# Where the window mask is added: two TensorE products a tile, or one VectorE addition in PSUM

## The chip, the cores and the metric

The kernel runs on one core of one Trainium2 chip. The metric is the device time of one execution, in microseconds (us). The time before is the median of three runs. A separate execution, taken with the hardware profiler, gave the profile and the trace. Engines are named as the profile names them: PE is TensorE (PEld its weight loads), DVE is VectorE, ACT is ScalarE, POOL is GpSimd, SP is SyncE, which here only issues DMAs.

## What is computed

The reference first runs a small decoder block over 2 x 512 tokens of width 128 (a Mamba scan, a mixture of experts and a cross-attention), and then six layers of windowed attention with a feed-forward network. The part that this change touches is the mask and the softmax of those six layers:

```python
q, k, v = split(x @ Wqkv)                       # 16 heads of 64
q = l2norm(q) * qs;  k = l2norm(k) * ksc        # then rotary position tables
bk2, bv2 = look(bk), look(bv)                   # windows of 32 tokens, each sees itself and the one before: 64 keys
mask = (it < jb) | (it > jb + w) | (jb == -1)   # later keys, keys over 32 back, keys before the start
sim  = einsum('bhwie,bhwje->bhwij', bq, bk2) * QK_SCALE
sim  = where(mask, -finfo.max, sim)
attn = softmax(sim, -1)
out  = einsum('bhwij,bhwje->bhwie', attn, bv2)  # then @ Wo, the residual and the feed-forward network
```

The mask has the same pattern for every head and every window, but for the first window of a sequence, in which the 32 keys of the window before do not exist.

## The kernel before

The first part (Mamba, experts, cross-attention; to about 376 us of the profile) is not changed, but for two ACT copies in its scan stage, which turn the mask constants into bf16, and one DMA that brings them in.

The six attention layers are cut into 48 tiles: 6 layers x 2 sequences x 4 tiles of 128 tokens (`ti` is the tile's number within its sequence, 0 to 3). Weights and constants lie in SBUF. The order of PE, ACT, DVE and POOL is written out by hand (L1434 to L1527): each engine works strictly in the order in which the steps are issued. Step s of the loop weaves together three tiles and the feed-forward network of a finished sequence:

- tile s, called A: `project` (q, k by PE into PSUM, L965), `rotate` (two DVE products from PSUM, L977 and L981, and a POOL addition, L986), `square` (ACT, L970) and `sums` (DVE, L990), `values` (PE L998, ACT copy to `va` L1000, DMAs to the shifted copy `vb`), `norm` (L1006 to L1015: the inverse square root by ACT's Ln and Exp, L930 and L931, a Newton step on POOL, L932 to L935, and POOL's two products with the rotated q and k, L1012);
- tile s-1, called B_: `flip_q` and `flip_k` (PE transposes L1147, ACT copies L1148), `scores` (L1032 to L1056), `softmax` (L1058 to L1064), `expo` (ACT, L1067);
- tile s-2, called C: `flip_p` (the weights transposed, L1147 and L1148), `attend` (PE L1086), `weigh` (DVE reciprocal L1100 and product L1101), `flip_o` (PE L1116, ACT L1118 and L1120), and, for every second tile, `out` (PE `wo_ps` L1137, DVE addition L1140);
- F1 and F2, the feed-forward network of a sequence whose four tiles are done: mean, variance (L1165), `spread` (L1177), `hidden` (L1216 to L1220), `out` (L1239), and ACT's table loads (L938 and L1204). They fall in three of each four steps.

PE's order within a step is: projection of q, flip_q, projection of k, flip_p, flip_k, attend, (hidden), values, scores, flip_o, (variance), (feed-forward out), attention out. While the first four steps run, pieces of the first part's end (`late(1)`) are woven between.

PSUM comes from two pools: "a", three buffers of two banks each (qk_ps, v_ps, sim, av), and "b", two buffers (transposes and outputs). Scores of a tile are a [128, 2, 4, 2, 64] tile of "a": 128 query rows, 16 heads, 64 keys.

`scores` first writes the mask: for each half of the PSUM tile, a product of `hot` (32 x 128 bf16, which says which of the 32 rows of a window a partition is) with `masks` (32 x 512 bf16) opens the accumulation with start=True (L1039). Then 64 small products of q and k, each 32 queries x 64 keys, are added to it with start=False (L1050). For ti = 0 the first of the two mask products takes the variant that also closes the first window's missing keys. `softmax` takes the maximum over the 64 keys (DVE, L1061) and subtracts it on the way from PSUM to SBUF (DVE, L1063); `expo` is ACT's Exp. The last tiles' work is finished by a written-out tail (L1530 to L1590).

Of the kernel before, what the change touches and what calls it, by code (L numbers as in the profile page):

```python
# [11 lines left out]
F32 = mybir.dt.float32  # L12
U32 = mybir.dt.uint32
I32 = mybir.dt.int32
BF16 = mybir.dt.bfloat16
# [6 lines left out]
B, S, D = 2, 512, 128  # L22
NT = B * S
P = 128
# [6 lines left out]
DEPTH, H, DH, WIN = 6, 16, 64, 32  # L31
# [5 lines left out]
NEG = -1e30  # L37
# [12 lines left out]


K_MASK = 0
K_HOT = K_MASK + 1024
K_HM1 = K_HOT + 128
K_HM2 = K_HM1 + 16
K_LT = K_HM2 + 128
K_TRI = K_LT + 64
# [9 lines left out]
def decoder_kernel(ctx: ExitStack, tc: tile.TileContext, t: dict, out: bass.AP):  # L67
    nc = tc.nc
    mm, tr = nc.tensor.matmul, nc.tensor.transpose

    const = ctx.enter_context(tc.tile_pool(name="const", bufs=1))
# [3 lines left out]
    lwb = ctx.enter_context(tc.tile_pool(name="lwb", bufs=1, side="right"))  # L75
# [11 lines left out]
    mhalf = const.tile([P, 1], F32, name="mhalf")  # L87
    nc.gpsimd.memset(mhalf, -0.5)

    hot = const.tile([WIN, P], BF16, name="hot")  # L90
    masks = const.tile([WIN, 2, S], BF16, name="masks")
    xT = const.tile([P, NT], F32, name="xT")

    tri = const.tile([P, P], BF16, name="tri")
# [13 lines left out]
    ps = front.enter_context(tc.tile_pool(name="fps", bufs=1, space=PSUM))  # L108
# [13 lines left out]
    def load(pool, shape, name, src):  # L122
        w = pool.tile(shape, F32, name=name)
        nc.sync.dma_start(out=w, in_=src)
        return w
# [11 lines left out]
    w_dt = load(sp, [DTR, DI], "w_dt", t["L0_attn_dt_proj_w"])  # L137
    cst = const.tile([P, NCST - K_HM1], F32, name="cst")
    nc.sync.dma_start(out=cst, in_=t["cst"][:, K_HM1:])
    stage = lwb.tile([WIN, K_HM1], F32, tag="wqkv", name="stage")  # L140
    nc.sync.dma_start(out=stage, in_=t["cst"][0:WIN, 0:K_HM1])
    w_o = load(fp, [P, 2, D], "w_o", t["L0_attn_out_proj_w"].rearrange("(c p) f -> p c f", p=P))
    w_r = load(fp, [P, NE], "w_r", t["L0_attn_router_w"])
    ctok = load(fp, [B * XK, D], "ctok", t["ctx_1024"].rearrange("b k d -> (b k) d"))
# [231 lines left out]
    def small(name, shape, dtype=F32, bufs=1):  # L376
        return ep.tile([P, *shape], dtype, tag=name, name=name, bufs=bufs)

    def sort(b):
# [12 lines left out]
        gt, eq = small("gt", [NTB, NE, NE]), small("eq", [NTB, NE, NE])  # L392
        lt = cst[:, K_LT - K_HM1 : K_LT - K_HM1 + 64].unsqueeze(1).to_broadcast([P, NTB, 64])
        eqv = eq.rearrange("p n e f -> p n (e f)")
# [418 lines left out]
    with tc.manual_schedule(engines={ET.PE, ET.Activation, ET.DVE, ET.Pool, ET.SP}):  # L813
        xn = norm_in(0)
        nc.scalar.activation(acol, cols[:, C_ALOG : C_ALOG + 2 * NS], AF.Exp)
        nc.gpsimd.tensor_scalar(acol, acol, -1.0, None, ALU.mult)
        turn_in(0, xn)
        xn = norm_in(1)
        p0, p1 = conv(0, 0), conv(0, 1)
        for hf, pm in enumerate((p0, p1)):  # L820
            nc.scalar.activation(xi[0][:, hf], pm, AF.Silu, bias=col(C_CONVB + hf))
        p0, p1 = gate(0, 0), gate(0, 1)
        for hf, pm in enumerate((p0, p1)):
            nc.scalar.activation(sz[0][:, hf], pm, AF.Silu)
        table("natural_log_exp_and_others")
        dt_b_c(0)
        turn_in(1, xn)
        halves = [delta(0, hf) for hf in range(2)]
        for g in halves:
            step(g)  # L830
        for hf, g in enumerate(halves):
            step(g)
            nc.vector.tensor_mul(dx[0][:, hf], dl[0][:, hf], xi[0][:, hf])

        def other_batch():

            p0, p1 = conv(1, 0), conv(1, 1)
            yield
            yield
            table("silu_and_others")  # L840
            for hf, pm in enumerate((p0, p1)):
                nc.scalar.activation(xi[1][:, hf], pm, AF.Silu, bias=col(C_CONVB + hf))
            p0, p1 = gate(1, 0), gate(1, 1)
            for hf, pm in enumerate((p0, p1)):
                nc.scalar.activation(sz[1][:, hf], pm, AF.Silu)
            table("natural_log_exp_and_others")
            yield
            yield
            dt_b_c(1)
            yield  # L850
            nc.scalar.copy(hot, stage[:, K_HOT : K_HOT + P])
            nc.scalar.copy(masks, stage[:, K_MASK : K_MASK + 2 * S].rearrange("p (a s) -> p a s", a=2))
            nc.scalar.copy(tri, cst[:, K_TRI - K_HM1 : K_TRI - K_HM1 + P])
            yield
            for hf in range(2):
                g = delta(1, hf)
                step(g)
                yield
                yield
                step(g)  # L860
                yield
            nc.gpsimd.tensor_mul(dx[1], dl[1], xi[1])

        third = {n for n in range(NS) if n % 3 == 2}
        weave(scan(0, third), other_batch())
        table("exp_and_others")
        e0, e1 = experts(0), experts(1)
        early = chain(route(0), sort(0), e0, combine(0), cross(0))
        beside = [0, 1, 3, 5, 7, 8, 10, 11, 13, *range(16, 32, 2)]
        tables = cross_tables()  # L870
        for i, _ in enumerate(scan(1, {n for n in range(NS) if n % 2 == 0})):
            if i in beside:
                step(early)
            elif i > 14:
                step(tables)
        for _ in tables:
            pass
        scans.close()
        lwa = ctx.enter_context(tc.tile_pool(name="lwa", bufs=1))
        for i, _ in enumerate(chain(route(1), sort(1), e1)):  # L880
            step(early)
            if i in (12, 14, 16, 18, 20):
                step(early)
        for _ in early:
            pass
# [56 lines left out]
    class Tile:  # L942
# [89 lines left out]
        def scores(self):  # L1032

            qT, kT = self.qT, self.kT
            ps = psa.tile([P, 2, 4, 2, 64], F32, tag="a", name="sim")
            for par in range(2):
                mm(  # L1039
                    ps[:, par].rearrange("p g s k -> p (g s k)"), hot,  # L1040
                    masks[:, 1 if self.ti == par == 0 else 0, :],
                    start=True, stop=False, skip_group_check=True,
                )
            for hg in range(4):
                for slot in range(2):
                    for c in range(2):
                        for par in range(2):
                            for r in range(2):
                                j, w = 2 * c + (r ^ par), 2 * slot + par
                                mm(  # L1050
                                    ps[32 * j : 32 * j + 32, par, hg, slot, :],
                                    qT[64 * r : 64 * r + 64, 2 * hg + c, WIN * w : WIN * (w + 1)],
                                    kT[64 * r : 64 * r + 64, 2 * hg + c, WIN * w : WIN * (w + 2)],
                                    start=False, stop=True, skip_group_check=True,
                                )
            self.ps = ps  # L1056

        def softmax(self):  # L1058
            p3 = self.ps.rearrange("p a g s k -> p (a g s) k")
            m = tmp.tile([P, 16], F32, tag="m", name="m")  # L1060
            nc.vector.tensor_reduce(m, p3, AX.X, ALU.max)  # L1061
            s = tmp.tile([P, 16, 64], F32, tag="s", name="s", bufs=1)
            nc.vector.tensor_sub(s, p3, m.unsqueeze(2).to_broadcast([P, 16, 64]))  # L1063
            self.sf = s.rearrange("p x k -> p (x k)")  # L1064
# [369 lines left out]
    with tc.manual_schedule(engines={ET.PE, ET.Activation, ET.DVE, ET.Pool}):  # L1434
        onto_z(0, xT[:, bs(0)])
        rest = late(1)
        for s in range(len(tiles)):
# [93 lines left out]
        a, b, c = (  # L1531
            Part(DEPTH - 1, 1, layers[DEPTH - 1], t0, w)
            for t0, w in ((0, 2 * P), (2 * P, P), (3 * P, P))
        )
# [78 lines left out]
def _cst():  # L1613
    c = np.zeros((P, NCST), np.float32)
    p = np.arange(P)
    q, key = np.arange(WIN), np.arange(64)

    off = q[:, None] + WIN - key[None, :]
    m = np.where((off < 0) | (off > WIN), NEG, 0.0)

    m = np.broadcast_to(m[:, None, None, None, :], (WIN, 2, 4, 2, 64)).copy()
    m[:, 1, :, 0, :WIN] = NEG
    c[:WIN, K_MASK : K_MASK + 1024] = m.reshape(WIN, 1024)
    c[:WIN, K_HOT : K_HOT + P] = q[:, None] == (p % WIN)[None, :]
    c[p, K_HM1 + p // 8] = 1.0
    c[:, K_HM2 : K_HM2 + P] = (p[:, None] % XH) == (p[None, :] // 8)
    e = np.arange(NE)
    c[:, K_LT : K_LT + 64] = (e[None, :] < e[:, None]).reshape(1, 64)
    c[:, K_TRI : K_TRI + P] = (p[:, None] < p[None, :]) / P
    c[:, K_ROW : K_ROW + P] = p[None, :] / P  # L1630
    c[:, K_NUM : K_NUM + NSL] = np.arange(NSL)[None, :]
    c[:, K_TOK] = p
    c[:, K_TOK + 1 : K_TOK + 5] = P * np.arange(4)[None, :]
    return c
# [83 lines left out]
```

## Time and profile before

| what | value |
|---|---|
| runs | 1294.85, 1301.05, 1294.79 us; median 1294.85 |
| the profiled execution | 1302.94 us; its span 1301.2 us |
| mean granted clock of PE | 0.942 |
| 0 to 376 us, first part | PE busy 277 us, DVE 249, ACT 130, POOL 190; clock 0.85 |
| 376 to 456 us, first tiles with the woven end of the first part | PE 61 of 80 us, DVE 57; clock 0.85 |
| 456 to 1223 us, tiles | PE 728 of 767 us; DVE 538, ACT 439, POOL 442; clock 1.00 |
| 1223 to 1302 us, the end | PE 40 of the first 44 us, 24 of the last 35 |
| mask products (L1039) | 96 of 384 ns, two a tile |
| scores (L1050) | 6144 PE records, 1.42 us a tile on the chain of waits |

A "busy" figure is the time in which an engine ran any instruction. In a group's row come the line, the engine, the operation, the tiles out<-in, the shape and the count; then the busy time, the mean time of one in ns, and the idle time of the engine just before it with what ended it. "issue" is time in which an engine waited for nothing that the profile shows. The chain of waits is the sequence of work that ended last, followed back from the end of the execution.

### The profile page before, as it was taken

Reading aid. Unit: us, or ns where it says so; the run is one execution under the profiler, and the core shown is the slowest. Engines: PE = TensorE matmul, PEld = TensorE weight load, DVE = VectorE, ACT = ScalarE, POOL = GpSimd, SP = SyncE. Lnnn points to the kernel's source line nnn. Section 1 sums busy time; section 2 is a strip of 40 time slices with the busy share of each in tenths; the row PEclk is TensorE's granted clock in tenths of the full one; section 3 lists DMA queues with packets and bytes.
Section 4 is the critical chain, followed back from the end, with each engine's and each line's share of the span. In section 5 each row is a group of like instructions: output and inputs, shape, how many; then the busy total and the mean of one; then the engine's idle time right before and its main releaser. Section 6 shows DMA issues by size and latency. Waiting matters only on the chain.

```text
span 1301.2 us, 37984 instructions
## 1 busy us (share of the span) xinstructions
PE 1130.2 (87%) x16629; PEld 733.6 (56%) x16629; DVE 885.0 (68%) x1198; ACT 639.0 (49%) x1126; POOL 695.0 (53%) x704
## 2 busy tenths in 40 slices
PE   6677678857857899999999999999999999899987
PEld 2223256756734666666656666666656565555666
DVE  2798867535587676777767676777767675766654
ACT  4534132313333456565656555565646555554643
POOL 2577574154352565646646464656646464555641
PEclk9888689869977999999999999999999999999998
DMA  3222364468310212111121112111121111101100
GB/s 114 75 65 81 120 194 149 125 185 275 109 46 18 73 40 80 36 45 41 36 79 51 30 40 79 52 42 34 30 79 52 31 35 31 36 18 31 36 15 18
DMA packets 51889, 88.52 MB, mean 68 GB/s; under 512 B 7086, under 2 KB 23852, under 8 KB 51724
## 3 DMA queue, kind: packets, MB, share of 16 engines
q1 hardware_dynamic: 46796, 76.78, 19.6%
q10 hardware_dynamic: 3456, 6.29, 1.7%
q0 software_dynamic: 1472, 3.02, 1.1%
q8 instruction: 131, 2.15, 0.7%
q14 instruction: 34, 0.28, 0.1%
HBM read 58.92 MB, written 3.19 MB: 48 GB/s over the span
## 4 chain that ended last, share of the span: by engine, by line
PE 60%; ACT 9%; DVE 8%; issue 5%; POOL 5%; DMA 0%; another core or an unknown queue 0%; POOLq 0%; DVEq 0%; ACTq 0%
PE qk_ps L965 11%; PE t_ps L1147 7%; PE wo_ps L1137 7%; PE v_ps L998 6%; PE av L1086 4%; PE sim L1050 4%; ACT pT L1148 2%; PE fo_ps L1239 2%; PE t_ps L1116 2%; PE gu_ps L542 2%; PE fg_ps L1216 2%; PE sim L1039 2%; ACT oT L1118 1%; PE fa_ps L1217 1%; ACT sq L970 1%
## 5 line engine op out<-in xcount | busy, mean ns | idle before, releaser
L986 POOL TENSOR_TENSOR t<-t,t 128x1024 f32<-128x1024 f32 x94 | 222.7, 2371 | 155.3 <-DVE t L981 154.3
L965 PE MATMUL qk_ps<-wqkv,z 128*128 128x512 f32 x384 | 187.4, 612 | 0.8 <-ACT sq L970 0.4
L1012 POOL TENSOR_TENSOR t<-t,rn 128x1024 f32<-128x1024 f32 x94 | 177.2, 1907 | 3.7
L977 DVE TENSOR_TENSOR t<-qk_ps,tab 128x1024 f32<-128x1024 f32 x96 | 117.5, 1224 | 76.0 <-PE qk_ps L965 75.9
L1147 PE MATMUL t_ps<-ident,t 128*128 128x128 f32 x768 | 102.8, 277 | 25.0 <-ACT pT L1148 10.8
L1147 PEld LDWEIGHTS t_ps<-ident,t 128*128 128x128 f32 x768 | 87.1, 143 | 63.4 <-issue 36.5
L990 DVE TENSOR_REDUCE ss<-sq 128x16 f32<-128x1024 f32 x96 | 116.4, 1213 | 4.0 <-ACT sq L970 0.2
L1009 POOL TENSOR_SCALAR ss<-ss 128x32 f32<-128x32 f32 x47 | 13.4, 285 | 196.8 <-ACT sc L1008 196.8
L981 DVE TENSOR_TENSOR t<-qk_ps,tab 128x1024 f32<-128x1024 f32 x96 | 116.6, 1215 | 0.0
L1148 ACT COPY qT<-t_ps 128x512 f32<-128x512 f32 x96 | 51.7, 588 | 126.8 <-PE t_ps L1147 126.7
L1061 DVE TENSOR_REDUCE m<-sim 128x16 f32<-128x1024 f32 x48 | 58.8, 1225 | 69.5 <-PE sim L1050 69.5
L970 ACT ACTIVATE sq<-qk_ps 128x1024 f32<-128x1024 f32 x96 | 97.7, 1036 | 12.8 <-DVE t L981 12.8
L965 PEld LDWEIGHTS qk_ps<-wqkv,z 128*128 128x128 f32 x384 | 69.6, 197 | 52.6 <-issue 49.6
L998 PE MATMUL v_ps<-wqkv,z 128*128 128x512 f32 x192 | 93.8, 611 | 0.0
L1137 PE MATMUL wo_ps<-oT,wo 128*128 128x256 f32 (+1 forms) x400 | 89.5, 378 | 3.3 <-ACT oT L1118 3.3
L1086 PE MATMUL av<-va,pT 64*32 64x65 f32 x3072 | 83.9, 228 | 8.9 <-issue 8.9
L314 PE MATMUL y<-hs,ident 128*128 128x512 f32 x128 | 77.4, 741 | 15.5 <-DVE hs L334 9.4
L293 ACT ACTIVATE da<-dl,acol 128x512 f32<-128x512 f32 x64 | 43.8, 690 | 88.5 <-DVE hs L326 60.0
L1086 PE MATMUL av<-vb,pT 64*32 64x65 f32 x3072 | 83.1, 228 | 2.9 <-DVE ln_xc L1198 2.4
L1137 PEld LDWEIGHTS wo_ps<-oT,wo 128*128 128x128 f32 x400 | 73.7, 194 | 19.5 <-ACT oT L1118 6.3
L542 PE MATMUL gu_ps<-xT,w 128*128 128x128 f32 x480 | 72.1, 303 | 11.6 <-ACT xT L535 4.0
L1148 ACT COPY pT<-t_ps 128x512 f32<-128x512 f32 x96 | 51.6, 589 | 62.0 <-PE t_ps L1147 62.0
(351 smaller groups left out, 2323.5 us busy)
## 6 DMA issues: line engine op xcount, KB each, us to landing
w<-in_experts_dram SPq DMA_DIRECT2D x90, 256.0 KB
vb<-va SPq DMA_DIRECT2D x48, 390.0 KB
wqkv<-in_L_ffn_Wqkv_dram SPq DMA_DIRECT2D x18, 512.0 KB
vb<-va SPq DMA_DIRECT2D x36, 130.0 KB
b_sb<-bcd SPq DMA_DIRECT2D x16, 256.0 KB
b_sb<-bcd ACTq DMA_DIRECT2D x16, 256.0 KB
wo<-in_L_ffn_Wo_dram SPq DMA_DIRECT2D x6, 512.0 KB
c_sb<-bcd ACTq DMA_DIRECT2D x8, 256.0 KB
```

The lines of the kernel that those rows point to most:

```text
L965: mm(pa[:, hf * S : (hf + 1) * S], self.xb, w[:, w0 : w0 + S], start=True, stop=True)
L970: nc.scalar.activation(sq.rearrange("p h d -> p (h d)"), self.raw[qk], AF.Square)
L977: nc.vector.tensor_mul(t1, pa.rearrange("p (h d) -> p h d", d=DH), tab[:, 2 * qk, ti, :].unsqueeze(1).to_broadcast([P, H, DH]),)
L981: nc.vector.tensor_mul(t2.rearrange("p h (x d) -> p h x d", x=2), swap_halves(pa), tab[:, 2 * qk + 1, ti, :].rearrange("p (x d) -> p x d", ...
L986: self.calc.tensor_add(t1, t1, t2)
L990: nc.vector.tensor_reduce(self.ss[:, qk], self.sq[qk], AX.X, ALU.add)
L998: mm(pv[:, hf * S : (hf + 1) * S], self.xb, w[:, w0 : w0 + S], start=True, stop=True)
L1012: self.calc.tensor_mul(self.rot[qk], self.rot[qk], self.rn[:, qk].unsqueeze(2).to_broadcast([P, H, DH]),)
L1086: mm(po[hh][32 * at : 32 * at + 32, g, i * DV : (i + 1) * DV], pT[rows, 4 * par + hg, 32 * j : 32 * j + 32], (self.v if par else self.v2)[ ...
L1137: mm(po, wo_l[:, c, :], self.oT[:, c, at : at + w], start=c == 0, stop=c == INNER // P - 1)
L1147: tr(pt[:, n, :], src[:, (4 * g + n) * P : (4 * g + n + 1) * P], ident)
L1148: nc.scalar.copy(dst[:, 4 * g : 4 * g + 4, :], pt)
```

## The change

The mask is no longer a product. The two mask products a tile are gone from `scores`, and each of the 64 score products now writes PSUM by itself (start=True). `softmax` gains one DVE addition ahead of the maximum, in place in PSUM: the scores plus a mask tile from SBUF, read again for every head by a broadcast. For ti > 0 the same 64 values of a partition serve all 16 groups; for ti = 0 the form with 128 values in each half is used, where the first window's mask has the missing keys closed. The constants change with it: `masks` is now [128, 2, 2, 64] in f32, loaded from HBM by one DMA (128 x 256 values), in the place of the DMA of the bf16 masks' f32 source (32 x 1152 values); the ACT copies that made `hot` and `masks` are gone. In the two kernels as built, the orders of instructions on all engines agree otherwise: PE has 96 products and 96 weight loads fewer, DVE 48 additions more, ACT two copies fewer, POOL the same, SP the one DMA replaced.

The Newton step on POOL, which the change's title names as well (`self.calc`, L932 to L935), is in both kernels.

```diff
-    hot = const.tile([WIN, P], BF16, name="hot")
-    masks = const.tile([WIN, 2, S], BF16, name="masks")
+    masks = const.tile([P, 2, 2, 64], F32, name="masks")
...
-    stage = lwb.tile([WIN, K_HM1], F32, tag="wqkv", name="stage")
-    nc.sync.dma_start(out=stage, in_=t["cst"][0:WIN, 0:K_HM1])
+    nc.sync.dma_start(out=masks, in_=t["cst"][:, 0:K_HM1].rearrange("p (a s k) -> p a s k", a=2, s=2))
...
-            nc.scalar.copy(hot, stage[:, K_HOT : K_HOT + P])
-            nc.scalar.copy(masks, stage[:, K_MASK : K_MASK + 2 * S].rearrange("p (a s) -> p a s", a=2))
...
             ps = psa.tile([P, 2, 4, 2, 64], F32, tag="a", name="sim")
-            for par in range(2):
-                mm(
-                    ps[:, par].rearrange("p g s k -> p (g s k)"), hot,
-                    masks[:, 1 if self.ti == par == 0 else 0, :],
-                    start=True, stop=False, skip_group_check=True,
-                )
...
-                                    start=False, stop=True, skip_group_check=True,
+                                    start=True, stop=True,
...
         def softmax(self):
             p3 = self.ps.rearrange("p a g s k -> p (a g s) k")
+            if self.ti:
+                nc.vector.tensor_add(
+                    p3, p3, masks[:, 1, 0].unsqueeze(1).to_broadcast([P, 16, 64])
+                )
+            else:
+                p4 = self.ps.rearrange("p a g s k -> p a g (s k)")
+                nc.vector.tensor_add(
+                    p4, p4,
+                    masks.rearrange("p a s k -> p a (s k)").unsqueeze(2).to_broadcast([P, 2, 4, 128]),
+                )
             m = tmp.tile([P, 16], F32, tag="m", name="m")
             nc.vector.tensor_reduce(m, p3, AX.X, ALU.max)
```

More of the change, by code (lines that the diff above doesn't have):

```diff
@@ L52 @@
 K_MASK = 0
-K_HOT = K_MASK + 1024
-K_HM1 = K_HOT + 128
+K_HM1 = K_MASK + 256
 K_HM2 = K_HM1 + 16
@@ L1619, in _cst @@
     m = np.where((off < 0) | (off > WIN), NEG, 0.0)
[L1621 to L1624, printed above, removed]
+    m = np.broadcast_to(m[:, None, None, :], (WIN, 2, 2, 64)).copy()
+    m[:, 0, 0, :WIN] = NEG
+    c[:, K_MASK : K_MASK + 256] = np.tile(m.reshape(WIN, 256), (P // WIN, 1))
     c[p, K_HM1 + p // 8] = 1.0
```

## The prediction

> **What bounds the kernel now.** I read the table of engines first, then the windows of the tile stage, the chain of waits, DVE's groups and last PE's idle time.
>
> ```profile
> PE 1130.2 (87%) x16629; PEld 733.6 (56%) x16629; DVE 885.0 (68%) x1198; ACT 639.0 (49%) x1126; POOL 695.0 (53%) x704
> PE 60%; ACT 9%; DVE 8%; issue 5%; POOL 5%; DMA 0%; another core or an unknown queue 0%; POOLq 0%; DVEq 0%; ACTq 0%
> ```
>
> The window of the tile stage (stretch, its length, then busy us and instructions of PE, weight loads, DVE, ACT, POOL, and the clock):
>
> ```profile
> 456.00:1223.00 767.00, 727.87 (x13366) 472.80 (x13349) 537.99 (x617) 438.64 (x732) 441.52 (x465) 1.00 0.15 44
> ```
>
> PE is busy 727.87 of 767 us, 95%, at the full granted clock (1.00); DVE 538, 70%. So PE sets the pace, and PE work that goes is worth time wherever nothing else ends just behind it. What goes (L1039), and the rows nearest to what comes, in the groups by shape (busy us, mean ns | idle before):
>
> ```profile
> L1101 DVE TENSOR_TENSOR o<-av,rd 128x512 f32<-128x512 f32 x96 | 66.4, 692 | 3.3
> ...
> L1061 DVE TENSOR_REDUCE m<-sim 128x16 f32<-128x1024 f32 x48 | 58.8, 1225 | 69.5 <-PE sim L1050 69.5
> L1063 DVE TENSOR_TENSOR s<-sim,m 128x1024 f32<-128x1024 f32 x48 | 58.8, 1224 | 1.7
> ...
> L1039 PE MATMUL sim<-masks,hot 32*128 32x512 bf16 x96 | 29.2, 384 | 0.0
> ```
>
> The chain of waits over one tile (start, us, what):
>
> ```profile
> 606.64 1.91 POOL t L1012
> ...
> 608.60 1.09 PE t_ps L1147 x8
> ...
> 613.94 1.43 PE av L1086 x87
> 615.37 1.91 PE v_ps L998 x4
> 617.28 0.53 PE sim L1039 x2
> 617.81 1.42 PE sim L1050 x91
> ```
>
> The mask pair stands on the chain with 0.53 us. Once in four tiles the chain leaves PE: POOL's L1012 releases the flips (L1147).
>
> **Removed from PE.** 96 mask products. A pair lengthens the chain by 0.53, so at most 48 x 0.53 = 25.4 us. With its two weight loads a pair is four of PE's instructions; one event semaphore a tile comes in: counted in the two built programs, 147 less in all, about 3 a tile. This small count matters below.
>
> **Added on DVE.** 48 adds of 128x1024, PSUM plus an SBUF mask into PSUM. The nearest row reads PSUM and SBUF in one pass: L1063, 1.224 us. No row has DVE writing PSUM. Lower bound: the fixed part hidden. L1101 and L1063 give (1224-692)/512 = 1.04 ns an element and 0.16 us fixed, so 1.06. Upper bound: read and write in turn, 2x1.06+0.16 = 2.29. I take 1.22, as its shape is L1063's, and 1.26 with the gap between two DVE instructions. Scores end 0.53 earlier, so the softmax ends 1.26-0.53 = 0.73 later. The add waits for the last score; the maximum, subtraction, DVE's next rotations (L977, L981) queue behind it, expo (L1067) waits for them, and PE's flip_p for expo. The Trainium skill's page "VectorE: DVE Perf Modes", section "Rules for kernel authors", speaks against this: in a chain of DVE operations count matters, for each drains. By it the add costs DVE its full 1.2 us, never the 1.06; by the rows the cost is only what its followers can't wait for. So, by kind of tile (n mod 4):
>
> - n=1 and n=3: DVE is idle 4.1 and 6.7 us before the next rotation, and L1012 ends 4.1 and 5.8 us before flip_q needs it. All hidden: 0.53 gained each.
> - n=2: the timeline of one such tile, DVE's and ACT's, is tight.
>
> ```profile
> 638.67 1.22 DVE L1063 TENSOR_TENSOR s<-sim,m 128x1024 f32<-128x1024 f32 x1
> 641.45 1.22 DVE L977 TENSOR_TENSOR t<-qk_ps,tab 128x1024 f32<-128x1024 f32 x1 [1.56 <-PE qk_ps L965]
> ```
>
> ```profile
> 640.27 1.04 ACT L1067 ACTIVATE s<-s 128x1024 f32<-128x1024 f32 x1
> 641.32 1.28 ACT L1204 ACT_TABLE_LOAD   x1
> ```
>
> L1063 ends at 639.89, with the add at 640.62, so expo starts 0.35 late (not 640.27); ACT's table load and flip_q's copies queue behind it, so flip_p starts at about 643.7 instead of 643.84. Gained: 0.14. The 1.56 idle before L977 absorbs the rest.
> - n=0: PE waits for va, Newton and L1012 (above), none of which moves against v_ps. Gained: 0. The first rotation comes 0.58 later, inside the 1.09 us that DVE idles before the second. Without that cover it would cost up to 0.58.
>
> One group of four gains 0.53+0.14+0.53 = 1.20. Tiles 5 to 47 are 10.75 groups: 12.9. The first four tiles run with PE waiting on the earlier part: net -0.1. The last tile's tail is bound by DVE: +0.7. Sum: -12.3 us. POOL is no worse beside more DVE work: L1012 takes 1.90 both beside the softmax and beside L977.
>
> **Setup.** Two ACT copies of the scan stage go (0.28 and 1.04 us at 52 us): ACT waits there for DVE afterwards, so 0. The mask DMA takes the place of the staging DMA in SP's queue, 128 KB for 144 KB: 0, since it is needed 300 us later; no other queue is passed.
>
> **What moves: PE's instruction pages.** PE's idle time in the waits view names no engine:
>
> ```profile
> PE av L1086 <- issue: 6.0, 4, 1.5
> PE sim L1050 <- issue: 4.9, 4, 1.6
> PE t_ps L1116 <- issue: 3.6, 4, 1.4
> ```
>
> ```profile
> 1116.05 0.21 PE L1086 MATMUL av<-va,pT 64*32 64x65 f32 x1 [1.48 <-issue]
> ```
>
> Counting PE's instructions in the trace, the stalls of the tile stage fall at numbers 15041, 17601, 20161, 22465, 24001 ... 31425: every one is 193 plus a multiple of 256. The instruction queue (q8) moved 131 packets, 2.15 MB, 16 KB each, one for each 256 of PE's 33,603 instructions. Each packet starts about 0.9 us after PE enters a page, and PE resumes some 2.5 us after that: a page that PE runs through in under 3.4 us stalls. The weighted values (256 instructions in 1.4 to 1.75 us) and the scores (1.42) do; a page of scores, flips and products takes longer. There are 14 such stalls of 0.4 to 1.7 us, 17.4 us. The Trainium skill's "Runtime: NRT & Kernel Launch", section "Instruction fetch mechanics", says that crossing a 16 KiB boundary costs a tail-bump, mostly hidden. By the page this term is 0 before and after, and the sum stays -12.3; by the trace it is 17.4 us of before and can change.
>
> Before, a group of four tiles is 2569 instructions, 10 pages and 9: the boundaries drift, so almost pure pages come up only now and then, from tile 20 on. After, it is 2557, 10 pages less 3: the boundaries nearly stand still, and where they stand decides. In the built program of after they stand badly. In all eleven n=1 tiles a page holds 227 to 256 products of attend (L1086): about 1.5 us each. The page behind it (rest of attend, v_ps, some 240 scores) lost 0.8 to 1.0 before and runs 0.5 shorter now: about 0.4 over the eleven. The n=3 tiles 7 to 31 have such a page too (237 to 255), about 1.1 each, and two later ones 0.5. Pages that split attend and scores in halves take 3.3 us: about 0.1 in 22 tiles. Sum: 16.5+4.4+7.7+1+2.2 = 31.8. What goes: 14 stalls, of which 14.3 lengthened their tiles' periods, and one drop of the clock behind a stall, 1.8: 16.1. Net +15.7.
>
> **Sum.** -12.3+15.7 = +3.4 on the profiled execution: 1302.94 us, its span 1301.2 and 1.7 around it, hence 1306.3. The median of the runs is 1294.85, 8.1 lower, perhaps because fetches are faster unprofiled. Both terms carried over, the stalls a little smaller: 1294.85+3 = 1298. With stalls half as large, +7.9-12.3 = -4: 1290.5.
>
> **Rivals.** First, nothing lasting stalls: page costs hide, as the skill has it, or the stalls belong to profiling. Then 1294.85-12.3 = 1282.5; if DVE's add hides everywhere, down to 1270. For it: PE's 95%. Against: 14 rows at exact multiples of 256.
>
> Second, slower: the standing pages stall in full on every attend in the n=1 and n=3 tiles. Place: the boundary before L1086. Price: 22 x 1.5 and 11 x 1.0 on the page behind = 44, less 16.1 and 12.3: +15.6 at worst, and +7 with the n=3 pages at half size; between them 1306. It decides from about 19 full stalls in all on (12.3+16.1 = 28.4 us at 1.5): fewer, and the change gains. Any clock drop behind a stall adds 1.8.
>
> Third: the add in place runs at 2.29. The extra 1.07 costs 0.93 at n=2 and, past 0.52 of cover, 0.55 at n=0, so a group is slower by 1.48-1.06 = 0.4 and stalls come on top: about 1314. Against: L1063 shows no cost for two operands.
>
> Fourth, it doesn't do what it says: excluded, as the built program has 48 more TensorTensor on DVE and 96 fewer matmuls.
>
> **How the numbers follow.** Likeliest, gain and stalls nearly cancelling (1290 to 1303): 0.50. Stalls hidden (1270 to 1288): 0.24. Full stalls (1302 to 1310): 0.20. Slow add (over 1308): 0.06. The range 1281 to 1307 leaves out half of the last two and the far end of the second. A measurement of this kernel can tell about 0.5% (6.5 us) from no change. Faster by more (under 1288.4): 0.25, the second case; slower (over 1301.3): 0.33, the last two and the upper end of the first; within: 0.42.
>
> **What would show it.** DVE's new row: 48 at about 1.22; over 1.6 speaks for the third. PE's busy time falls by about 25 us. The "issue" rows grow from 17 us to about 32, all at multiples of 256 plus 193, attend's in n=1 tiles first; if they don't, this step is wrong. "L1147 <- POOL L1012" stays at once in four tiles. The forecast fails if unprofiled fetches are much faster, or if DVE's later softmax makes PE wait in n=1 or n=3.

## The result and the profile after

The changed kernel takes 1302.05 us (median of 15 runs), the kernel before 1294.85. The ratio of all runs is 1.0047, with a 95% interval of 1.0025 to 1.007: slower by about 6 us (the two medians lie 7.2 apart). It lies in the forecast range (1281 to 1307 us), at the upper edge of the likeliest case (1290 to 1303).

The page of the changed kernel's profile: the span, then the busy time of each engine.

```profile
span 1296.5 us, 37894 instructions
...
PE 1118.8 (86%) x16533; PEld 732.1 (56%) x16533; DVE 942.8 (73%) x1246; ACT 637.7 (49%) x1124; POOL 694.7 (54%) x704
```

This profiled execution is 4.7 us *shorter* than the one of before, although the runs are longer. The two parts of the trace tell why. Scores of the first tile begin at 378.3 us in the trace of before and at 367.4 in this one; the kernels are alike up to there but for the constants, and over the eleven traces of this study that moment lies anywhere between 364.8 and 381.5 us. That part scatters from execution to execution, and only the stretch from the first score to the end belongs to the change. The windows of that stretch, before and then after (length, then busy us of PE, weight loads, DVE, ACT, POOL, and the clock):

```profile
378.29:1301.17 922.88, 852.97 (x15440) 560.59 (x15440) 634.09 (x796) 507.38 (x856) 503.18 (x544) 0.98 0.15 42
```

```profile
367.36:1296.48 929.12, 839.12 (x15346) 559.58 (x15346) 693.32 (x844) 506.98 (x856) 502.56 (x544) 0.98 0.14 42
```

PE is busy 13.9 us less, and the stretch is 6.2 us longer, which is what the runs say (0.0047 x 1295 = 6.1). So PE stands idle 20 us more. (A fall of about 25 us was forecast; the mask products did go, but scores take 4.9 us more in sum, the v_ps products 3.1 and the transposes 2.5.) The groups by shape show the new DVE operation, and the waits of PE from 366 us on show the idleness:

```profile
L1061 DVE TENSOR_REDUCE m<-sim 128x16 f32<-128x1024 f32 x48 | 58.8, 1224 | 1.7
L1063 DVE TENSOR_TENSOR s<-sim,m 128x1024 f32<-128x1024 f32 x48 | 58.8, 1224 | 1.6
...
L1051 DVE TENSOR_TENSOR sim<-sim,masks 128x1024 f32<-128x1024 f32 x36 | 44.4, 1232 | 31.1 <-PE sim L1040 31.0
...
L1056 DVE TENSOR_TENSOR sim<-sim,masks 128x1024 f32<-128x1024 f32 x12 | 14.8, 1231 | 25.9 <-PE sim L1040 25.9
```

```profile
PE av L1086 <- issue: 17.0, 13, 2.4
PE sim L1040 <- issue: 15.3, 12, 4.1
PE t_ps L1147 <- POOL t L1008: 13.0, 12, 2.4
```

The addition in place costs 1.23 us, like its neighbours. The maximum (L1061) had 69.5 us of idle time before it, waiting for scores; now it follows the addition at once. PE's two largest waits are of the kind "issue"; 4.1 us of the scores' row are the gap ahead of the very first score. Counted at the places where PE's instruction number is 193 plus a multiple of 256, so where one page of 256 instructions ends and the next begins, there are 26 gaps of over 0.2 us, 29.8 us in all, for 14 and 17.4 before. These are called stalls here. One of them on the chain of waits:

```profile
608.38 1.36 PE av L1086 x83
609.74 2.37 issue
612.11 0.32 PE av L1086 x8
612.43 3.15 PE v_ps L994 x4
615.58 1.69 PE sim L1040 x100
```

PE stands still for 2.37 us in the middle of attend, and what follows takes 3.15 us where it took 1.91 in the chain of before: the slower pace behind some stalls that the prediction counted once. It is the clock, as the windows around it show (the number behind POOL's is the granted share):

```profile
608.00:612.00 4.00, 1.72 (x122) 1.35 (x121) 2.36 (x4) 2.27 (x4) 4.00 (x2) 1.00 0.12 37
612.00:616.00 4.00, 3.89 (x47) 1.54 (x49) 2.02 (x3) 0.38 (x1) 0.06 (x1) 0.62 0.01 4
```

In the trace's clock record it stands at half for 3.41 us from 612.96 on. Of after's stalls from the fifth tile on, those of 2.37, 2.13 and 2.09 us have such a drop behind them, and one of 2.31 has none.

Tiles are counted from 1 here, so n=1 is the first tile of a sequence. The period of a tile runs from its first score to that of the next tile; the attend that comes just ahead of a tile's first score thus lies in the period of the tile before. The periods by kind of tile, where no stall falls in them (us):

| tile n mod 4 | before | after, undisturbed | forecast gain | gain |
|---|---|---|---|---|
| 1 | 18.04 | 17.51 | 0.53 | 0.53 |
| 2 | 20.40 | 20.13 | 0.14 | 0.27 |
| 3 | 19.69 | 19.15 | 0.53 | 0.54 |
| 0 | 14.00 | 14.00 | 0 | 0 |

### The profile page after: what moved, and what is told of

It reads as the page before. It is cut to its first block, busy times and chain, and to the rows that moved or that the text cites. A ratio compares the mean times of both kernels' runs of the same rounds, so it can differ in the third digit from the quotient of the medians.

```text
span 1296.5 us, 37894 instructions
## 1 busy us (share of the span) xinstructions
PE 1118.8 (86%) x16533; PEld 732.1 (56%) x16533; DVE 942.8 (73%) x1246; ACT 637.7 (49%) x1124; POOL 694.7 (54%) x704
## 3 DMA queue, kind: packets, MB, share of 16 engines
q8 instruction: 130, 2.13, 0.7%
## 4 chain that ended last, share of the span: by engine, by line
PE 58%; DVE 13%; ACT 11%; issue 5%; POOL 4%; DMA 1%; SPq 0%; POOLq 0%; DVEq 0%; ACTq 0%
PE qk_ps L961 8%; PE t_ps L1147 7%; PE wo_ps L1137 7%; PE v_ps L994 7%; PE av L1086 5%; PE sim L1040 4%; PE gu_ps L540 3%; ACT pT L1148 2%; PE fo_ps L1239 2%; PE y L312 2%; POOL t L1008 2%; PE fg_ps L1216 2%; PE xd L561 2%; PE fa_ps L1217 1%; PE t_ps L1116 1%
## 5 line engine op out<-in xcount | busy, mean ns | idle before, releaser
L1008 POOL TENSOR_TENSOR t<-t,rn 128x1024 f32<-128x1024 f32 x94 | 176.8, 1902 | 3.7
L1147 PE MATMUL t_ps<-ident,t 128*128 128x128 f32 x768 | 103.7, 278 | 32.5 <-POOL t L1008 13.0
L1147 PEld LDWEIGHTS t_ps<-ident,t 128*128 128x128 f32 x768 | 86.4, 143 | 71.8 <-issue 32.6
L994 PE MATMUL v_ps<-wqkv,z 128*128 128x512 f32 x192 | 96.8, 627 | 1.7 <-ACT kT L1148 1.1
L1040 PEld LDWEIGHTS sim<-kT,qT 64*32 64x32 f32 x6144 | 66.9, 107 | 54.1 <-issue 52.1
L1040 PE MATMUL sim<-kT,qT 64*32 64x64 f32 x6144 | 77.9, 230 | 16.1 <-issue 15.3
L1067 ACT ACTIVATE s<-s 128x1024 f32<-128x1024 f32 x48 | 50.8, 1058 | 82.1 <-DVE s L1063 82.1
```

Source lines behind the costliest of these rows:

```text
L994: mm(pv[:, hf * S : (hf + 1) * S], self.xb, w[:, w0 : w0 + S], start=True, stop=True)
L1008: self.calc.tensor_mul(self.rot[qk], self.rot[qk], self.rn[:, qk].unsqueeze(2).to_broadcast([P, H, DH]),)
L1040: mm(ps[32 * j : 32 * j + 32, par, hg, slot, :], qT[64 * r : 64 * r + 64, 2 * hg + c, WIN * w : WIN * (w + 1)], kT[64 * r : 64 * r + 64, 2 ...
L1147: tr(pt[:, n, :], src[:, (4 * g + n) * P : (4 * g + n + 1) * P], ident)
```

## The experiments

The theory to be tested: the change gains about 1.3 us in four tiles, and loses it again because it moves the 256-instruction pages of PE to where they stall. The rivals: the stalls belong to profiling, or DVE's later softmax is what the runs pay for. A third, that any idle product at the start changes the time, wherever the pages stand, is tested by the last two runs. The lever is a number of idle products on PE. They write PSUM that a later product overwrites, and put nothing else in another order; each is four PE instructions.

```diff
+    def pads(pt, n):
+        for k in range(n):
+            j = 32 * (k % 4)
+            mm(pt[j : j + 32, 0:64], ident[0:64, 0:32], ident[0:64, 0:64], start=True, stop=True)
...
         pt = bank(name)
+        if name == "nT_ps0":
+            pads(pt, 42)
```

**168 instructions (a168).** 

> The kernel after, with 42 idle products (168 PE instructions, [64x32] by [64x64] of the identity, into PSUM that the first transposes overwrite) at PE's start, where it waits 8 us for its first data. Nothing else moves, but every boundary of PE's pages of 256 instructions stands 168 instructions earlier in the tiles: between halves of attend and scores, no longer at their ends. Page theory: of some 27 stalls (30 us in the trace of after) all but a few go, stalls left under 5 us, time about 25 to 28 below after: ratio to before about 0.983 (1273 us). Rival, the stalls belong to profiling or the added DVE operation is what costs: ratio as after, 1.0047, within 0.3%.

Measured: 1.0333 (1.0305 to 1.0362), slower by 37 us than after, where I had expected 25 faster. The rival allowed 0.3% around after, so it fell; but so did my rule for where the stalls fall. There were 45.9 us of stalls. (A gap of 3.84 us in the first tile also stands at such a number, but it is the wait for kT that the kernel before has there too.) PE's waits in this kernel (attend is now L1093, scores L1047):

```profile
PE av L1093 <- issue: 29.2, 19, 1.9
PE sim L1047 <- issue: 21.4, 18, 4.0
```

The chain of waits of one n=2 tile shows a page that my rule called safe:

```profile
479.23 0.86 PE ln_mean L1160 x2
480.08 0.88 PE t_ps L1154 x8
480.96 1.72 PE qk_ps L968 x4
482.68 0.45 PE t_ps L1154 x4
...
483.15 0.59 ACT pT L1155
...
483.88 1.06 PE t_ps L1154 x8
484.94 0.25 PE av L1093 x8
...
485.20 1.11 PE av L1093 x68
486.32 1.36 issue
487.67 0.46 PE av L1093 x30
```

PE entered this page at 478.63 and left it at 486.32: 7.7 us, far over my 3.4. Yet its packet on the instruction queue started only at 485.35, 6.7 us after the entry and not 0.9; PE resumed 2.3 us after that. No other instruction packet was moved in the 9 us before it, so the request was late, not the queue busy. Here a page of slow transposes and then attend asked late and ran out early.

The clock adds to it. Over tiles 5 to 46 a168 takes 34.1 us more than after. Its gaps are 20.3 us longer, and its granted clock stands at half for 37.5 us, in nine drops behind gaps of 1.6 to 1.9 us, for 6.8 us in after; at half speed the 30.7 us more are worth about 15 (my estimate).

**96 instructions (a96, the same edit with 24 products).** 

> The same with 24 idle products (96 instructions). By the page theory the boundaries now leave the n=1 and n=3 tiles and stand at the ends of attend in the n=2 and n=0 tiles: about as much stalls as in after (26 us worked out from its trace), in other tiles. n=0 waits for POOL anyway and hides part: ratio to before 0.998 to 1.006. Rival, the idle products themselves help or hurt (a warmer clock, a later start): then it goes the way of the run with 168, at about 96/168 of its size.

Measured: 1.0102 (1.0059 to 1.0145), above the expected 0.998 to 1.006, with 34.0 us of stalls. They moved to the n=2 and n=0 tiles as expected. The rise over after is 0.55%, where the rival, by the number of products, makes it 1.6%.

**The kernel before with 112 + 88 instructions (b112j88; flip takes a count and calls pads on its first PSUM tile).** 

> The kernel before, with 28 idle products at PE's start (112 instructions) and 22 more (88) ahead of flip_q of tile 29, where PE waits for POOL anyway. By the page theory its drifting boundaries then miss the attend and score bursts: 14 stalls become about 3, 17 us about 3, and the clock drop goes: ratio to before 0.988 to 0.990 (about 1280 us). Rival: no change, 1.000. Against the run of after with 168 it gives the worth of the change without stalls: after should be 10 to 13 us below (0.990 to 0.992) if the sum without stalls was right, equal if the DVE addition eats the gain.

Measured: 1.0159 (1.0132 to 1.0186), with 24 stalls of 32.3 us instead of 3. The same wrong rule: its boundaries stood in pages of flips and attend.

**168 instructions without the addition (n168).** 

> The run with 168, with the DVE additions left out: no mask is applied at all. It prices the added operation where it stands. My sum: 0 in n=1 and n=3 tiles, about 0.25 to 0.4 in n=2, 0 in n=0, 0.7 to 1.3 in the tail: 3 to 5 us below the run with 168. Rival, the addition is on the path of every tile: 48 x 1.26 less 48 x 0, up to 60 us below.

Measured: 1.0248 (1.0214 to 1.0282), 0.85% or 11 us below a168, with 50.5 us of stalls: too much stands on the stalls for a price of the addition. Inconclusive, but 60 us are excluded.

From these six traces I read off, for each kind of tile, how far from the first score a boundary stalls: where attend and its weights' flips lie. The next runs used these zones, so they test them on kernels from which they were not read.

**56 instructions (a56, 14 products).** 

> The kernel after with 14 idle products (56 PE instructions) at PE's start. The traces of the six kernels so far show where a page boundary stalls: at distances of -55 to 0 instructions from the first score in n=1 tiles, -81 to 13 in n=2, -99 to 13 in n=0 (the flips ahead of attend delay the fetch as well), some at -55 to -30 in n=3. A shift of 56 keeps all four kinds out of these zones but for the first n=0 tiles. Revised page theory (the place of the boundary decides, the place is to be read from traces): stalls in the tiles 1 to 3 us instead of 27, time 22 to 26 us below after: ratio to before 0.984 to 0.988. Rival (any idle products at the start slow the kernel down, as all four did so far): above 1.0047.

Measured: 0.9803 (0.9778 to 0.9829), 1268.0 us. This is 2.4% below after, a little more than expected, and faster than the kernel before: the version that beats both. (Part of its lead over before are before's own 17.4 us of stalls.) The window from its first score to the end, and PE's "issue" waits:

```profile
372.43:1272.30 899.87, 832.39 (x15346) 557.21 (x15346) 693.05 (x844) 507.83 (x856) 502.63 (x544) 0.98 0.15 43
```

```profile
PE sim L1047 <- issue: 5.1, 4, 4.2
PE t_ps L1123 <- issue: 4.4, 3, 2.0
```

The same 844 DVE and 15,346 PE instructions as in after take 29.3 us less. (4.2 us of the scores' row are again the gap ahead of the first score.) What stalls are left (9.6 us) lie mostly in n=0 tiles, where PE would have waited for POOL: from the eighth tile on their period stays 14.0 but for one of 14.19; only the fourth tile's is longer, 16.41. Of the 29.1 us that tiles 5 to 46 lose, 18.3 are gaps and about 3.4 the two drops of the clock, which are gone; the other 7 I did not trace.

**The kernel before with jumps (bj: no products at the start, 34 ahead of flip_q of tile 17 and 17 ahead of that of tile 33).** 

> The kernel before with no products at the start, but 34 idle products (136 instructions) ahead of flip_q of tile 17 and 17 (68) ahead of that of tile 33, chosen by the same zones so that its drifting boundaries miss them. Revised page theory: of 14 stalls (17 us) one or two are left, ratio to before 0.986 to 0.990. Against the run of after with 56, without stalls in either, after should be lower by the gain of the mask products alone, 12 to 14 us (about 1%). Rival, the change is worth nothing or costs without stalls: both equal.

Measured: 0.9974 (0.9958 to 0.999). Eight stalls of 9.4 us were left, for the one or two expected; four of them, of 1.26 to 1.68 us before the n=2 tiles 18, 22, 26 and 30, stand 87 to 114 instructions ahead of the first score, further out than my zone reached. In tiles without stalls its periods are those of before (18.03, 20.40, 19.68, 14.00); the 17 products ahead of tile 33 cost nothing, and the period with the 34 is 14.99, with a stall of 0.30 in it. The run missed its range, so the table above gives the gain without stalls better than these two times do.

**56 instructions without the addition (n56).** 

> The run with 56 without the DVE additions: no mask is applied. It prices the addition with hardly any stalls around: by the periods of the trace of after, 0.25 a tile in n=2 and 0 in the others, and 0.7 to 1.3 in the tail: 3 to 5 us below the run with 56 (ratio to it 0.996 to 0.998). Rival, DVE's later softmax is on the path in most tiles: 10 us or more below.

Measured: 0.9769 (0.9742 to 0.9797), 0.35% or 4.4 us below a56, by the two medians 5.4; the two intervals overlap, so the size is rough, but 10 us would be too much. Of the undisturbed periods only that of n=2 falls, from 20.13 to 19.88: 2.8 us over its eleven tiles from the sixth on. The rest is not where I had put it. The tail, from the last tile's first score on, does not fall (39.34 and 39.50 us in the two traces). The second tile does, from 26.51 to 24.48 (with 168 instructions from 25.90 to 24.50): there the end of the first part is woven in, and the second half of flip_o waits once more for ACT. The first two lines are of a56, the third is of n56:

```profile
415.07 0.66 PE L1123 MATMUL t_ps<-ident,o 128*128 128x128 f32 x4 [0.68 <-ACT late_p L1415]
416.40 1.11 PE L1123 MATMUL t_ps<-ident,o 128*128 128x128 f32 x4 [0.67 <-ACT oT L1125]
409.58 1.09 PE L1113 MATMUL t_ps<-ident,o 128*128 128x128 f32 x8 [0.68 <-ACT late_p L1405]
```

**256 and 312 instructions (a256, a312: 64 and 78 products).** 

> The kernel after with 64 idle products at PE's start: 256 instructions, exactly one page, so that every page boundary of the tiles stands where it stands in after. Page theory: ratio to before as after, 1.0047 within 0.3%, with the same stalls (27 us) at the same tiles. Rival, the number of idle products (warmth of the clock, a later start of PE, one more fetch) made the runs with 56 faster and with 96 and 168 slower: something else, and near the run with 312.

> The kernel after with 78 idle products: 312 instructions, one page and 56, so that the boundaries stand as in the run with 56. Page theory: ratio to before 0.980 as there, within 0.4%, although only 14 products more are added than in the run with 256. Rival: as the run with 256.

Measured: 1.0045 (1.0023 to 1.0066) and 0.9791 (0.9768 to 0.9815). A whole page more changes nothing: after had 1.0047, a56 0.9803. Fourteen products more, from 64 to 78, are worth 2.5%. PE's waits of a256, from behind its first score on, are again those of after:

```profile
PE av L1093 <- issue: 15.1, 12, 2.2
PE t_ps L1154 <- POOL t L1015: 12.6, 12, 1.6
...
PE sim L1047 <- issue: 10.6, 13, 1.6
```

64 idle products leave the place of the boundaries and the time as they were, and 14 more change both: that the place of the boundary decides is shown, by time and by trace, and the number of products is ruled out.

## Why the prediction was right, and where it was not

**The gain on PE** was as forecast at n=1, n=3 and n=0. At n=2 it was 0.27 and not 0.14: expo did start about 0.3 late, but flip_p with it lost only 0.27 of the 0.53, where I had counted 0.39. Over tiles 5 to 46 the undisturbed periods fall by 14.2 us; my -1.20 a group made 12.6 of it. At n=0 the 0.53 turned into waiting for POOL, as the step said: that wait (L1147 for L1012, L1008 after) grew from 5.6 us in 7 places to 13.0 in 12.

**The addition** took 1.232 us for the 1.22 taken; the in-place write to PSUM took no second pass, so the third rival fell. Its place was right at n=2, and n56 prices it at roughly 4.4 us for the 3 to 5 that follow. That the total fits is in part luck: it is n=2 and the second tile, not n=2 and the tail. The advice of the Trainium skill's page "VectorE: DVE Perf Modes" (section "Rules for kernel authors") to minimize the count of chained operations, which the prediction read as one more operation at its full time, holds for DVE's busy time (59 us more) and says nothing of the kernel's.

**The stalls** were the step that decided the sign. In tiles 5 to 46 the periods exceed the undisturbed ones by 15.8 us before (16.1 taken) and 32.1 after (31.8 taken). That the total agrees is luck, for its parts do not: pages of attend at n=1 cost 13.1 (16.5 taken), the pages behind them 13.3 (4.4 taken), those at n=3 5.4 (8.7 taken), and the pages that split attend and scores nothing (2.2 taken). These costs contain the drops of the clock. The rule by which I placed them, a page stalls when PE runs through it in under 3.4 us since its packet starts 0.9 us after entry, is the step that failed. In the first experiment it was wrong by 60 us. The packets of before already spoke against it: of the 121 from the first score on, ten start before PE enters the page, by up to 2.4 us, and some 25 over 1.5 us after the entry. For pages that begin with attend the rule comes near enough, and after's boundaries stand there; that carried its sum.

**Left out** were stalls in the first four tiles: they take 98.7 us instead of 95.2. The first is 2.1 shorter, the second 2.0 longer (the addition's price there, as n56 shows it), the third the same, and the fourth, with a stall of 1.8 us, 3.7 longer. I had forecast -0.1. The tail rose by 0.7 as forecast, but its stalls rose by as much (from 1.73 to 2.44 us), so this doesn't show that the addition costs 0.7 there.

**The balance** of the tile stretch: -14.2 and +16.3 in tiles 5 to 46, +3.6 in the first four, +0.6 at the end, hence +6.2. I had +3.4. The prediction laid the 8.1 us between the profiled execution of before and the median to fetches that are faster unprofiled; the first part alone scatters by 16.7 us over the eleven traces, which is enough for it. The section "Instruction fetch mechanics" of the Trainium skill's page "Runtime: NRT & Kernel Launch" has such crossings "mostly hidden". By count they are, in after some hundred of 130; the 26 that are not cost 29.8 us, and the timed runs move by what the traces say, so this is no effect of profiling.

**Open** is what releases the request for a page. In the sixteen of a168 that came over 4 us after the entry, the packet started 0.6 to 1.6 us after ACT's second copy of pT had ended, the last one that attend needs; but other packets of that trace start up to 2.5 us before PE enters their page, and no single position in the page fits all. The zones are read off, not explained. Open is also why the clock drops behind some stalls and not behind others as long.

## What to carry to other kernels

When an edit adds or removes instructions on an engine that runs through 256 small ones in about 1.5 us, as PE does here, count its instructions modulo 256 before and after, and look in the trace for gaps that name no engine at equal distances in that count. Judge such an edit with the phase held fixed or swept, since the phase here was worth more than the edit: 2.4% against 1.1% of gain. And take a difference of two profiles stretch by stretch: the part that the change did not touch differed by 11 us.

## What was not expected of the hardware

The time of one and the same kernel spans 0.979 to 1.033 of before by 14 to 78 idle products at its start. A page crossing costs PE up to 2.4 us, and can cost twice: behind one such stall the granted clock fell to half for 3.4 us, and a v_ps group took 3.15 us for 1.91; in a168 such drops are worth nearly as much as its longer gaps. A DVE addition that reads and writes the same PSUM took 1.232 us for 1024 elements, against 1.224 with SBUF as its destination.
